# A graph attention and expert kernel: edge lists per pair of nodes instead of per node, with a buffer for every row tile

## The chip, the cores and the metric

The kernel runs on one core of a Trainium2 chip. The metric is the device time in microseconds (us) of one execution; lower is better. The engines named below are TensorE (PE; its weight loads are shown as PEld), VectorE (DVE), ScalarE (ACT), GpSimd (POOL) and SyncE (SP). Each takes its own instructions in order. DMA transfers are issued from SP, ACT and POOL, and those that gather rows by an index held in memory come from POOL.

## The reference, cut to what matters

1250 nodes with 768 features pass through two graph attention layers over 41250 edges (20000 drawn ones in both directions and one loop per node; the edges come sorted by destination), each layer adding a further loop per node, and then through a transformer block with attention and a routed mixture of experts.

```python
def _gat_layer(x, W, a_src, a_dst, b, src, dst, n_nodes):
    h = x @ W
    e_src = h @ a_src
    e_dst = h @ a_dst
    e = leaky_relu(e_src[src] + e_dst[dst], 0.2)
    m = segment_max(e, dst, num_segments=n_nodes)
    w = exp(e - m[dst])
    z = segment_sum(w, dst, num_segments=n_nodes)
    alpha = w / z[dst]
    return segment_sum(h[src] * alpha[:, None], dst, num_segments=n_nodes) + b

gnn = gat(relu(gat(layernorm(x), ...)), ...)      # two layers
x = x + gnn
x = x + ffn(layernorm(x))                         # attention, then 8 experts, 2 per row
```

The change lies wholly in the part ahead of the first layer's weighted sum.

## The kernel before, in words

**Counts instead of edges.** The kernel never sums over edges. It makes a dense table `cnt[source, destination]` of how often each edge occurs (125 x 10 x 1250, 16-bit) and uses it as a factor of a dense weight matrix. Nodes are cut into ten tiles of T = 125. The features of the nodes, layer-normalised, are held transposed in `xT`.

**How the lists are found.** Every edge gets a key, destination x 1250 + source (`key`, 125 rows of 330). The keys are stored to a DRAM array `keys`, with a tail of large values behind them. For a node, `find_rows` counts with a comparison (`begun`) and a one-column product (`pk`) in which row of 330 keys its edges start; `gather_row` fetches that row of keys for each of 125 nodes by an indirect DMA of POOL (`kr`); `first_edges` counts on DVE how many keys of the row lie before the node, and gathers the next SL = 64 keys from there (`win`). So there is one list of 64 per node, and each tile of 125 nodes costs two indirect DMAs. `gather_row` runs LEAD = 3 tiles ahead.

**How the lists become counts.** Two tiles at a time are transposed (`pl`), which gives 128 partitions (two lists of 64) by 625 columns (`lt`). A source node is split into tile number (`jb`) and place in the tile (`pb`); for the second list of a column the tile number is shifted by 10 (`shift`). For groups of PG = 25 columns DVE compares `pb` with 0 to 127 (`ohp`, 128x3200) and, every fifth group, `jb` with 1 to 20 (`ohj`, 128x2500); PE then makes, for every column, one product of the two (`pc`, 128x20), 25 to a group, 25 groups. ACT copies each group into `cnt`, one copy for each of the two lists (L423). `ohp` and the product's PSUM tile have two buffers each. If a list doesn't hold all the edges, a loop (L434) counts them in another way instead; with the drawn edges it makes no turn.

**What else goes on there.** A row tile of x is loaded (`xn`, four buffers; in a 112-row and a 13-row piece), its mean and spread are taken (`spread`), it is normalised (`normal`, on ACT), transposed on PE (`ptr`, six products of 128x125) and copied into `xT` (`columns`). The weight W1 (`gw`) is loaded in one DMA of 2304 KB. Three of the ten tiles of h = xW (`ph`, `project`, EARLY = 3) are computed between the row tiles, and seven after the counts. Of the scores e_src and e_dst only the vectors W a are formed: `attention_vectors` multiplies the six chunks of W with the vector spread over all partitions (`rep`) on DVE and sums (`scr`, twelve instructions, result `wa1`), one or two after each tile's list. `attention_terms` multiplies `wa1` with `xT` on PE (`pe`, three column chunks of six products), twelve before the counts and the rest one after every fourth group of counts; `pec` brings the result to rows (`es`).

**After the counts** the ones of the loops are added (L454), a mask `am` and the row maximum `most` are formed on DVE, transposed (`pmx`), turned into factors (`pes`, `rows`), and ten weight tiles `wt` are made on ACT and DVE; with them and h the weighted sum `pagg` starts.

**The order** on PE, DVE and POOL is written out by hand up to the end of the row tiles, and on PE and DVE in the counts (`manual_schedule`); elsewhere a scheduler orders them. Operations marked `keep_in_program_order`, some DMAs here, are not moved.

```python
for t in range(NT):
    if 2 <= t <= 7:
        spread(t + 2)
    first_edges(t)
    if t + LEAD < NT:
        gather_row(t + LEAD)
    if t % 3 == 0 and t // 3 < EARLY:
        project(xT, gw, h, gpo, [t // 3])
    vector(0 if t < 3 else 1 if t < 5 else 2)
    if 2 <= t <= 7:
        normal(t + 2)
        columns(t + 2)
```

Of the kernel before, what the change touches and what calls it, by code (L numbers as in the profile page):

```python
# [27 lines left out]
def gnn_ffn_kernel(  # L28
# [39 lines left out]
    SL = 64  # L68
    NP = N // 2
    PG = 25  # L70
# [9 lines left out]
    assert EC * T == E and EC % EB == 0 and 2 * SL == P and T % PG == 0 and NT % 2 == 0  # L80
# [79 lines left out]
    with tc.tile_pool(name="cnt", bufs=1) as cpool:  # L160
# [11 lines left out]
        def attention_vectors(layer, w, a_src, a_dst, pool, bufs, tags=("rep", "scr")):  # L172

            def load(a):
                rep = pool.tile([P, D], F32, tag=tags[0], name="rep", bufs=bufs if layer == 0 else None)
                tc.keep_in_program_order((nc.sync if bufs > 1 else nc.scalar).dma_start(
                    rep, bass.AP(tensor=a.tensor, offset=a.offset, ap=[[0, P], [1, D]])))
                return rep

            reps = [load(a) for a in (a_src, a_dst)[:bufs]]  # L180
            if bufs > 1:
                yield None
            for i in range(2):
                if i == bufs:
                    reps.append(load(a_dst))
                for c in range(DC):
                    scr = pool.tile([P, D], F32, tag=tags[1], name="scr", bufs=1 if layer == 0 else None)
                    nc.vector.scalar_tensor_tensor(scr, w[:, c, :], 1.0, reps[i], op0=ALU.mult, op1=ALU.mult,
                                                   accum_out=wa1[:, c, i:i + 1] if layer == 0 else wa2[:, i, c:c + 1])
                    yield None  # L190

        def attention_terms(xT, psum):

            for c0, w in CHUNKS:
                pe = psum.tile([P, 4, P], F32, tag="tr", name="pe").rearrange("p a b -> p (a b)")
                for c in range(DC):
                    g = c % 4
                    nc.tensor.matmul(pe[32 * g:32 * g + 32, :w], wa1[:, c, :], xT[:, c, c0:c0 + w],
                                     start=(c < 4), stop=(c + 4 >= DC))
                    if c == DC - 1:  # L200
                        nc.scalar.copy(er[:, c0:c0 + w], pe[:, :w])
                    yield None
# [17 lines left out]
        LEAD = 3  # L220
        with tc.tile_pool(name="edge", bufs=1) as ep, \
                tc.tile_pool(name="onehot", bufs=2) as op, \
                tc.tile_pool(name="epc", bufs=2, space=PSUM) as epc, \
                tc.tile_pool(name="gpt0", bufs=2, space=PSUM) as gpt, \
                tc.tile_pool(name="gpo0", bufs=2, space=PSUM) as gpo:

            ri = ep.tile([T, 2, EC], I32, name="ri")
            for i, (eng, a) in enumerate(((nc.sync, dst), (nc.scalar, src))):
                eng.dma_start(ri[:, i, :], a.rearrange("(p e) -> p e", p=T))
            xrows = []  # L230
            for t in range(4):
                xn = op.tile([T, D], F32, tag="xn", name="xn", bufs=4)
                split_rows(nc.sync if t % 2 == 0 else nc.scalar, xn, x[t * T:(t + 1) * T, :])
                xrows.append(xn)
            key = ep.tile([T, EC], F32, name="key")
            nc.vector.scalar_tensor_tensor(key, ri[:, 0, :], float(N), ri[:, 1, :], op0=ALU.mult, op1=ALU.add)
            tail = ep.tile([1, SL], F32, name="tail")
            nc.vector.memset(tail, 2.0 * N * N)
            nc.scalar.dma_start(keys[E:E + SL].rearrange("(o e) -> o e", o=1), tail)
            tc.keep_in_program_order(nc.sync.dma_start(keys[0:E].rearrange("(p e) -> p e", p=T), key))  # L240
            gw = wpool.tile([P, DC, D], F32, tag="w", name="gw1")
            tc.keep_in_program_order(nc.sync.dma_start(gw, gW1.rearrange("(c p) f -> p c f", p=P)))
# [6 lines left out]
            node = ep.tile([T, NT], F32, name="node")  # L249
            nc.gpsimd.iota(node, pattern=[[T, NT]], base=0, channel_multiplier=1,  # L250
                           allow_small_or_imprecise_dtypes=True)
            nc.vector.tensor_scalar(node, node, float(N), None, ALU.mult)
# [8 lines left out]
            shift = ep.tile([P, 1], F32, name="shift")  # L261
            nc.gpsimd.memset(shift, 1.0)
            nc.gpsimd.memset(shift[SL:P], 1.0 + NT)


            begun = ep.tile([T, N], BF16, name="begun")
            oneb = ep.tile([T, 1], BF16, name="oneb")
            nc.vector.memset(oneb, 1.0)
            row = ep.tile([T, NT], I32, name="row")
            edges = ep.tile([T, NT], F32, name="edges")  # L270
            at = ep.tile([T, NT], I32, name="at0")
            win = ep.tile([T, NT, SL], F32, name="win")
            krows = {}

            def find_rows():
                nc.vector.tensor_scalar(begun, nodes, head, None, ALU.is_gt)
                pk = epc.tile([P, 512], F32, tag="pc", name="pk")
                for t in range(NT):
                    nc.tensor.matmul(pk[:T, t:t + 1], begun[:, t * T:(t + 1) * T], oneb,
                                     start=True, stop=True)  # L280
                return pk

            def gather_row(t):
                krows[t] = op.tile([T, EC], F32, tag="kr", name="kr", bufs=LEAD)
                nc.gpsimd.indirect_dma_start(
                    out=krows[t], out_offset=None, in_=keys[0:E].rearrange("(p e) -> p e", p=T),
                    in_offset=bass.IndirectOffsetOnAxis(ap=row[:, t:t + 1], axis=0))

            def first_edges(t):

                count = small.tile([T, 1], F32, tag="count", name="count")
                nc.vector.scalar_tensor_tensor(key, krows[t], node[:, t:t + 1], ones[:T, :],
                                               op0=ALU.is_lt, op1=ALU.mult, accum_out=count)
                nc.vector.tensor_tensor(at[:, t:t + 1], count, edges[:, t:t + 1], ALU.add)
                nc.gpsimd.indirect_dma_start(
                    out=win[:, t, :], out_offset=None, in_=keys.rearrange("(e o) -> e o", o=1),
                    in_offset=bass.IndirectOffsetOnAxis(ap=at[:, t:t + 1], axis=0))
# [10 lines left out]
            xT = big.tile([P, DC, N], F32, tag="A", name="xnT")  # L308
            h = node_rows("h1")

            stats = {}

            def spread(t):
                if t == len(xrows):
                    xn = op.tile([T, D], F32, tag="xn", name="xn", bufs=4)
                    split_rows(nc.sync if t % 2 == 0 else nc.scalar, xn, x[t * T:(t + 1) * T, :])
                    xrows.append(xn)
                stats[t] = ln_root(xrows[t])

            def normal(t):  # L320
                mean, sd = stats.pop(t)
                rstd = small.tile([T, 1], F32, tag="rstd", name="rstd")
# [15 lines left out]
            with tc.manual_schedule(engines=fixed):  # L338
# [14 lines left out]
                for t in range(4):  # L353
                    columns(t)
# [755 lines left out]
```

## Time and profile before

| what | value |
|---|---|
| median of three runs (lowest, highest) | 1528.72 us (1525.68, 1529.65) |
| the profiled execution's own time, its span | 1527.86 us, 1526.1 us |
| PE, DVE, ACT, POOL busy of the span | 94%, 53%, 39%, 28% |
| first `ohj`, end of the last count copy | 70.29 us, 131.22 us |
| first `ph` after the counts, first `pagg` | 132.68 us, 195.61 us |
| `ph` products: 240 tile products' records, before and after the counts | 72 and 168 |

The span is the time from the first to the last instruction of one profiled execution, so it is a little shorter than that execution's own time. Busy shares are averages over stages with different limits. A group in the page is one source line on one engine: with its count, its busy time, the mean of one in ns, the idle time just before it and what ended that. The two records of one 32-bit product are counted singly, so that a `ph` tile of twelve products has 24 records.

### The profile page before, as it was taken

How to read it: one execution, taken by the hardware profiler on the slowest of the kernel's cores; microseconds unless marked ns; L12 is line 12 of the kernel's file. 1: busy time of each engine (PE TensorE's matmuls, PEld its weight loads, DVE VectorE, ACT ScalarE, POOL GpSimd, SP SyncE). 2: the span in 40 equal slices, each digit the busy share in tenths (PEclk: the TensorE clock that was granted, in tenths of full speed). 3: DMA queues.
4: the chain of work that ended last, by engine and by line, in shares of the span. 5: the costliest groups of instructions: out<-in, count | busy, mean ns of one | idle time of the engine just before them, and what ended most of it. 6: DMA issues, size and time to landing. Idle time of an engine off the chain costs nothing.

```text
span 1526.1 us, 15935 instructions
## 1 busy us (share of the span) xinstructions
PE 1442.0 (94%) x5957; PEld 781.8 (51%) x5957; DVE 813.5 (53%) x1326; ACT 598.0 (39%) x949; POOL 433.7 (28%) x288
## 2 busy tenths in 40 slices
PE   5699999999999999999999999999989996899998
PEld 3476655556555555553343343344333664566665
DVE  4797655435036650128778778778787764111111
ACT  3321613205116521236646646646656344221211
POOL 6300000000000010006646656655657222122222
PEclk9856999999999999999999999999999997899999
DMA  7100010000031129920000000000120433855644
GB/s 216 33 2 12 11 73 0 1 19 14 0 103 41 61 82 395 407 100 1 21 0 1 21 1 21 1 21 1 29 73 1 143 112 113 299 169 174 223 152 143
DMA packets 48848, 125.50 MB, mean 82 GB/s; under 512 B 6103, under 2 KB 22680, under 8 KB 48768
## 3 DMA queue, kind: packets, MB, share of 16 engines
q1 hardware_dynamic: 30958, 55.99, 11.0%
q0 software_dynamic: 12688, 57.10, 10.0%
q10 hardware_dynamic: 5122, 11.36, 2.6%
q8 instruction: 48, 0.79, 0.2%
q14 instruction: 32, 0.26, 0.1%
HBM read 71.30 MB, written 57.60 MB: 84 GB/s over the span
## 4 chain that ended last, share of the span: by engine, by line
PE 71%; DVE 9%; issue 8%; DMA 6%; ACT 4%; POOL 1%; POOLq 0%; SPq 0%; ACTq 0%; DVEq 0%
PE pagg L542 12%; PE ph L209 9%; PE st L694 8%; PE pav L738 7%; PE pk L657 5%; PE pv L673 5%; PE phe L1024 5%; PE poe L1033 5%; PE pq L657 4%; PE pc L419 2%; DMA xd<-yn,slot 2%; DVE sT L724 2%; PE po L882 2%; ACT sT L697 1%; DVE most L703 1%
## 5 line engine op out<-in xcount | busy, mean ns | idle before, releaser
L730 POOL TENSOR_TENSOR acc<-acc,sT 125x834 f32<-125x834 f32 (+1 forms) x139 | 273.0, 1964 | 10.9
L542 PE MATMUL pagg<-h,wt 125*125 125x385 f32 (+1 forms) x800 | 263.5, 486 | 0.4 <-DVE wt L535 0.4
L703 DVE TENSOR_TENSOR most<-most,st 125x834 f32<-125x834 f32 (+1 forms) x144 | 147.0, 1021 | 107.2 <-ACT sT L697 103.4
L542 PEld LDWEIGHTS pagg<-h,wt 125*125 125x125 f32 x800 | 147.1, 187 | 104.6 <-DVE wt L535 3.5
L724 DVE TENSOR_TENSOR sT<-sT,mb 125x834 f32<-125x834 f32 (+1 forms) x180 | 174.2, 1016 | 22.6 <-PE mb L719 22.6
L725 ACT ACTIVATE sT<-sT 125x834 f32<-125x834 f32 (+1 forms) x180 | 158.4, 900 | 49.3 <-DVE sT L724 49.0
L697 ACT COPY sT<-st 125x834 f32<-125x834 f32 (+1 forms) x180 | 151.5, 848 | 53.2 <-PE st L694 51.2
L694 PE MATMUL st<-qk 64*125 64x417 f32 (+1 forms) x720 | 164.9, 558 | 4.3 <-DVE most L703 4.2
L738 PE MATMUL pav<-sT,v 125*64 125x417 f32 (+1 forms) x720 | 151.8, 534 | 9.5 <-ACT sT L725 9.5
L635 POOL MEMSET zero<- 128x772 f32 x1 | 0.7, 741 | 505.9 <-PE ptr L140 505.9
L730 POOL TENSOR_TENSOR acc<-sT 125x834 f32<-125x834 f32 (+1 forms) x18 | 35.3, 1962 | 277.0 <-ACT sT L725 277.0
L694 PEld LDWEIGHTS st<-qk 64*125 64x125 f32 x720 | 56.9, 185 | 99.7 <-issue 43.2
L738 PEld LDWEIGHTS pav<-sT,v 125*64 125x64 f32 x720 | 42.8, 137 | 106.3 <-issue 43.8
L1033 PE MATMUL poe<-we,hT 128*128 128x384 f32 x264 | 88.8, 486 | 0.0
L657 PE MATMUL pq<-yT,wqk 128*128 128x417 f32 (+1 forms) x216 | 88.1, 534 | 0.0
L1037 DVE SCALAR_TENSOR_TENSOR sofar<-poe,weight,sofar 128x768 f32<-128x768 f32 x25 | 25.4, 1017 | 117.0 <-PE poe L1033 109.4
L882 PE MATMUL po<-wp,aT 128*125 128x384 f32 x240 | 87.5, 498 | 0.0
L209 PE MATMUL ph<-gw,xnT 128*125 128x384 f32 x240 | 85.5, 517 | 2.1 <-DVE cnt L454 2.1
L1024 PE MATMUL phe<-xT,we 128*128 128x384 f32 (+1 forms) x288 | 86.6, 460 | 0.0
L657 PE MATMUL pk<-yT,wqk 128*128 128x417 f32 (+1 forms) x216 | 84.0, 526 | 0.0
L673 PE MATMUL pv<-wv,yT 128*125 128x384 f32 x240 | 79.9, 490 | 1.4 <-issue 1.4
L546 DVE RECIPROCAL rz<-pagg 125x1 f32<-125x1 f32 x20 | 3.3, 166 | 141.5 <-PE pagg L542 141.5
(224 smaller groups left out, 1813.4 us busy)
## 6 DMA issues: line engine op xcount, KB each, us to landing
xd<-zero POOLq DMA_DIRECT2D x8, 3860.0 KB, 47.1
we<-in_L_ffn_W_dram SPq DMA_DIRECT2D x16, 1152.0 KB
xr<-xd SPq DMA_DIRECT2D x25, 386.0 KB
gw<-in_L_gnn_W_dram SPq DMA_DIRECT2D x2, 2304.0 KB
wqk<-in_L_ffn_Wqkv_dram SPq DMA_DIRECT2D x12, 384.0 KB
xres<-in_x_dram SPq DMA_DIRECT2D x10, 375.0 KB
xsd<-xres ACTq DMA_DIRECT2D x10, 375.0 KB
wv<-in_L_ffn_Wqkv_dram SPq DMA_DIRECT2D x1, 2304.0 KB
```

The lines of the kernel that those rows point to most:

```text
L209: nc.tensor.matmul(po[:, s, :DH], xT[:, c, t * T:(t + 1) * T], w[:, c, s * DH:(s + 1) * DH], start=(c == 0), stop=(c == DC - 1))
L542: nc.tensor.matmul(po[:, s, :DH + s], ws[j][:, (d - d0) * T:(d - d0 + 1) * T], h[:, j, s * DH:(s + 1) * DH + s], start=(j == 0), stop=(j = ...
L657: nc.tensor.matmul(pq[:, :w], wqk[:, c, i, :], yT[:, c, c0:c0 + w], start=(c == 0), stop=(c == DC - 1))
L694: nc.tensor.matmul(st[:T, i, :w], self.qk[r, 1, j * T:(j + 1) * T], self.qk[r, 0, self.c0:self.c0 + w], start=True, stop=True)
L697: nc.scalar.copy(s[:, :, :w], st[:T, :, :w])
L703: nc.vector.tensor_tensor(self.most[:, :, :w], prev[:, :, :w], st[:T, :, :w], ALU.max)
L724: nc.vector.tensor_tensor(s[:, :, :w], s[:, :, :w], self.mb[:T, :, :w], ALU.subtract)
L725: nc.scalar.activation(s[:, :, :w], s[:, :, :w], AF.Exp)
L730: nc.gpsimd.tensor_tensor(self.acc[:, :, :w], prev[:, :, :w], s[:, :, :w], ALU.add)
L738: nc.tensor.matmul(self.pav[r, :w], v[:, j, hd0:hd0 + HD], s[:, i, :w], start=(j == 0), stop=(j == NT - 1))
L1024: nc.tensor.matmul(ph[:, :n * P], w1[:, c, f * P:(f + 1) * P], xT[:, c, :n * P], start=(c == 0), stop=(c == DC - 1))
L1033: nc.tensor.matmul(po[:, d, :DH], hT[:, f, s * P:(s + 1) * P], w2[:, f, d * DH:(d + 1) * DH], start=(f == 0), stop=(f == FC - 1))
```

## The change

Every list now belongs to a pair of neighbouring nodes and has SL = 128 places. There are NU = 5 sets of 125 pairs instead of ten of 125 nodes. A source in a pair's list already carries the second node's offset of ten tiles, so `shift` is dropped, and a group's counts are copied to `cnt` in one copy of 50 columns instead of two of 25. All five `kr` gathers are issued at once.

Row tiles of x and gathered key rows have a buffer each, in a pool that closes before the counts. Edge lists and the key store are each sent in a 112-row and a 13-row piece (`queue`); the key store moves from SP's queue to ACT's, behind row tile 1; W1 stands on SP's queue behind row tiles 0, 2 and 3; row tiles 4 to 9 follow it there. `op`, the pool of the comparisons, opens after the row tiles, and `rep` is loaded then. The row tiles, lists and `ph` products are written in another order. `attention_vector` and `attention_terms` for layer 1 stand behind the counts and the loops' ones.

```diff
-    SL = 64
+    SL = 128
+    NU = NT // 2
...
+        def attention_vector(layer, i, w, rep, pool, tag):
+            for c in range(DC):
+                scr = pool.tile([P, D], F32, tag=tag, name="scr")
+                ins = nc.vector.scalar_tensor_tensor(
+                    scr, w[:, c, :], 1.0, rep, op0=ALU.mult, op1=ALU.mult,
+                    accum_out=wa1[:, c, i:i + 1] if layer == 0 else wa2[:, i, c:c + 1])
+                if layer == 0:
+                    tc.keep_in_program_order(ins)
...
+            def queue(eng, o, i):
+                for rs in (slice(0, 112), slice(112, T)):
+                    tc.keep_in_program_order(eng.dma_start(o[rs], i[rs]))
...
             for i, (eng, a) in enumerate(((nc.sync, dst), (nc.scalar, src))):
-                eng.dma_start(ri[:, i, :], a.rearrange("(p e) -> p e", p=T))
...
-            tc.keep_in_program_order(nc.sync.dma_start(keys[0:E].rearrange("(p e) -> p e", p=T), key))
-            gw = wpool.tile([P, DC, D], F32, tag="w", name="gw1")
-            tc.keep_in_program_order(nc.sync.dma_start(gw, gW1.rearrange("(c p) f -> p c f", p=P)))
+                queue(eng, ri[:, i, :], a.rearrange("(p e) -> p e", p=T))
...
+            with tc.tile_pool(name="early", bufs=1) as xp:
+                xrows = [xp.tile([T, D], F32, name=f"xn{t}") for t in range(NT)]
+                krows = [xp.tile([T, EC], F32, name=f"kr{u}") for u in range(NU)]
+                queue(nc.scalar, xrows[1], x[T:2 * T, :])
+                queue(nc.scalar, rows, key)
+                for t in (0, 2, 3):
+                    queue(nc.sync, xrows[t], x[t * T:(t + 1) * T, :])
+                tc.keep_in_program_order(nc.sync.dma_start(gw, gW1.rearrange("(c p) f -> p c f", p=P)))
+                for t in range(4, NT):
+                    queue(nc.sync, xrows[t], x[t * T:(t + 1) * T, :])
...
+                    for u in range(NU):
+                        nc.gpsimd.indirect_dma_start(
+                            out=krows[u], out_offset=None, in_=rows,
+                            in_offset=bass.IndirectOffsetOnAxis(ap=row[:, u:u + 1], axis=0))
...
+                    for t in range(4, NT):
+                        if t < 4 + NU:
+                            first_edges(t - 4)
+                        spread(t)
+                        if t > 4:
+                            normal(t - 1)
+                        if t % 2 == 0:
+                            project(xT, gw, h, gpo, [t // 2 - 2])
+                        if t > 4:
+                            columns(t - 1)
+                    normal(NT - 1)
+                    columns(NT - 1)
...
+            op = edge.enter_context(tc.tile_pool(name="onehot", bufs=2))
+            reps = [every_partition(a, op, "rep", nc.sync) for a in (ga_src1, ga_dst1)]
...
-            nc.vector.tensor_scalar(jb, jf, shift, good, ALU.add, ALU.mult)
+            nc.vector.tensor_scalar(jb, jf, 1.0, good, ALU.add, ALU.mult)
...
-                    u, q0 = divmod(g * PG, T)
-                    for i in range(2):
-                        c0 = (2 * u + i) * T + q0
-                        nc.scalar.copy(cnt[:, :, c0:c0 + PG],
-                                       pc[:T, :, i * NT:(i + 1) * NT].rearrange("p q j -> p j q"))
-                    if g % 4 == 3:
-                        next(terms, None)
-            for _ in terms:
-                pass
+                    c0 = 2 * g * PG
+                    nc.scalar.copy(cnt[:, :, c0:c0 + 2 * PG],
+                                   pc[:T].rearrange("p q (i j) -> p j (q i)", i=2))
...
             for t in range(NT):
                 d = cnt[:, t, t * T:(t + 1) * T]
                 nc.vector.tensor_tensor(d, d, ident[:T, :T], ALU.add)
+            for i, a in enumerate(reps):
+                attention_vector(0, i, gw, a, op, "scr")
+            attention_terms(xT, gpt)
```

## The prediction

> **What bounds the kernel now.** I read the chain of waits first, cut to the first 200 us (start, length, who holds the chain): everything the change touches lies ahead of the first `pagg` at 195.61 us, and behind it both programs issue the same work.
>
> ```profile
> 28.58 1.20 POOL win L295
> 29.78 0.30 issue
> 30.08 1.49 POOL kr L285
> ...
> 33.38 5.51 DMA kr<-keys,row
> ...
> 48.77 9.85 PE ph L209 x24
> ...
> 62.32 3.01 PE pe L198 x24
> ...
> 81.09 1.52 PE pe L198 x2
> ...
> 165.29 30.32 PE ph L209 x94
> 195.61 16.14 PE pagg L542 x50
> ```
>
> Three stretches. Up to 70.29 us (first `ohj`) the chain goes round between POOL, DMA and DVE, and PE is fed late. From there to 131.22 us it alternates between `ohp` (DVE) and `pc` (PE), with `pe` thrown in. From 132.68 to 195.61 us it is PE alone. The windows (busy us of each engine, granted clock, DMA share, GB/s) show their limits:
>
> ```profile
> 21.00:28.00 7.00, 7.00 (x23) 4.29 (x24) 1.21 (x4) 0.93 (x2) 3.11 (x3) 1.00 0.91 201
> 70.00:131.00 61.00, 53.93 (x637) 44.47 (x637) 53.71 (x32) 16.45 (x51) 0.00 (x0) 0.50 0.01 1
> ...
> 139.00:196.00 57.00, 56.99 (x205) 34.94 (x205) 36.62 (x53) 25.05 (x41) 0.00 (x0) 1.00 0.03 8
> ```
>
> In the second row PE and DVE are each busy 54 of 61 us, so neither hides the other; PE has half the clock. In the third PE is full while DVE has 20 us free. The timeline gives the hand-over between them:
>
> ```profile
> 131.64 2.08 DVE L454 TENSOR_TENSOR cnt<-cnt,ident 125x125 uint16<-125x125 uint16 x10 [3.85 <-ACT cnt L423]
> 132.51 0.50 ACTq L484 DMA_DIRECT2D bias<-in_L_gnn_b_dram  x1
> 132.68 0.49 PEld L209 LDWEIGHTS ph<-gw,xnT 128*125 128x125 f32 x2 [2.24 <-issue]
> ```
>
> PE takes up `ph` 1.46 us after the last count is copied out. That start is what the change moves.
>
> **What the Trainium skill says.** "TensorE: Matmul & The Clock Gate", section on the HAM clock gate: the array falls to half clock after an idle window of about 3.4 us and needs a busy one to come back. The trace agrees: 0.50 in 46 to 52 us after PE's pauses, 0.50 through the counts, back at 138.1 us, 5.4 us after `ph` starts. Same page, architectural detail: DVE and ACT are strictly first in, first out; so an operation queued ahead of what PE needs holds it. "DMA: Bandwidth & Descriptors", "Why a DMA increments its semaphore by 16": a copy takes the largest k up to 16 that divides its outer dimension, so 125 rows use 5 engines and 112 use 16. No row splits a transfer by engine, but one-piece `ri` lands only at 7.5 us. Same page, "Issuing engines are not separate DMA queues": all share the 16 engines; the trace agrees, the gathers land after 4.2 us at best and 10.8 at worst, when they run against `gw`.
>
> **The change, part by part.** Durations are of the profiled execution, span 1526.10 us, own time 1527.86, 0.86 below the median of the three runs, 1528.72; I add the difference to the median.
>
> 1. Start. `ri` (2 x 161 KB) and the key store go out in 112 and 13 rows. `key` starts at 7.54 now; estimate 5.0 (bounds 5.0 to 7.5). The key store leaves SP (issued at 9.58, 1.5 after `key` is done) for ACT's queue behind x row 1: about 6; ACT issues seven loads and stores ahead of its first activation instead of six, 0.3 to 0.4 more, while it waits for DVE's first `mv` anyway. First gather at 14.96 now, estimate 10 to 11.4. On SP `gw` now stands behind six pieces of x rows 0, 2, 3 (0.3 to 0.4 each, and the waits for earlier loads): issue at about 8 against 9.89. Rows 4 to 9 follow it on SP without waiting for buffers (now issued at 15.4 to 45.8).
>
> 2. Lists. Five `kr` (1.28) and five `win` (1.21) gathers fewer: POOL 12.5 us less; DVE 5 x (0.56 + 0.08 + 0.16) = 4.0 less. Half the bytes of `kr` (825 KB), the same bytes of `win`. `begun` halves (0.87 to about 0.5 to 0.9, strided), five `pk` fewer (0.12 each). This frees the chain of 28 to 47 us: DVE then needs neither 12 `scr` (12.0) nor ten lists before the last row.
>
> 3. The front on PE, by its own order: four tiles of transposes, `ph` 0, row 4, `ph` 1, rows 5 and 6, `ph` 2, rows 7 to 9, `psum`, `pl`. `gw` is 2304 KB; at 400 GB/s it lands near 17 to 18, at the 201 GB/s of the window in which gathers run, nearer 22. I take `ph` 0 at 20 (21.56 now). One `ph` tile is 24 records of 30.32 / 94 = 0.323 = 7.75 us warm (now 8.2, 9.2 and 10.0, two of them after a pause and partly at half clock). 20.0 + 7.75 + 0.6 cold = 28.3; row 4, 1.2; `ph` 1 to 37.3; rows 5 and 6 with their evictions, 2.1; `ph` 2 to 47.2; rows 7 to 9, 3.7: 50.9. From `pl` to `ohj` stays 66.33 to 70.29 = 3.96. `ohj` starts at **54.9 instead of 70.29: 15.4 less** (11 to 18).
>
> 4. Counts. Twelve `pe` products (3.01) leave the front, six of 1.52 leave the counts, 9.1 us of PE. What remains on PE, 25 x 1.85 = 46, is below DVE's 25 x 1.89 + 5 x 1.46 = 54.5; so DVE bounds: 54.5 + last `pc` 1.86 + copy 0.6 + hand-overs 0.5 = 57.4 against 60.93: **3.5 less** (1.5 to 4). Fifty count copies of 0.32 become 25 of about 0.57 (an ACT copy of 125x500, `rows`, takes 0.57); ACT is at 16 of 61 us, so only the last one shows. `rf` (0.49) moves to a DVE that waits for PE anyway.
>
> 5. Behind the counts. Let T be the end of the last copy, 131.22 now. DVE: diagonal until T+2.5, then the twelve `scr`, which DVE issues ahead of all else, at 1.00 each (204.84, 205.84 in layer 2): T+14.5. PE issues all 18 `pe` ahead of the remaining `ph`; the first needs the seventh `scr`, the sixth the twelfth. So 168 `ph` records stand behind DVE. Then 12 `pe`, 3.0 warm to 6 at half clock; `er` copy and the last `pec`, 1.5. `ph` starts at about T+20.5 (19.3 to 22.3), not T+1.46. What follows: 168 x 0.323 = 54.2, and `pmx` and `pes` as now, 139.00 to 195.61 less 160 records and `pec`, 3.6: `pagg` at T+78.3 against T+64.4: **13.9 more** (12.7 to 16). DVE's own chain, ten `am` ahead of `es`, `most`, then the first `wt` row, ends near T+57, inside that. `rep` now loads after the x rows have left their buffers, near 50 us, and is wanted at about 115: the counts, with DMA at 1 GB/s, hide it; without them it would cost 3 to 5 us.
>
> Sum: -15.4 - 3.5 + 13.9 = -5.0; 1526.1 becomes 1521.1, the execution 1522.9, the median 1523.7.
>
> **The rivals.** *A draw.* With both gathers and loads at 200 to 220 GB/s the front gains only 11, the counts 2.5, and PE's stall costs 15: +1.5; or kinder, 12.5, 3 and 14: -1.5. For it: 201 GB/s at a DMA share of 0.91 above. Against it: half the gather bytes. It gives 1526 to 1530.
>
> *Slower: the gathers starve.* DVE's order puts the first list's count, which waits for `krows[0]`, ahead of row 4's statistics. Rows 0 to 9, `gw` and five gathers now compete from 8 us on. If `kr` lands at L, row 4 is ready for PE at L + 0.8 + 1.25 + 0.8 + 1.25 + 0.6 + 1.0 = L + 5.7; PE wants it at 28.3, so each us of L beyond 22.6 is lost. At 27.6 the gain is gone, from 32.2 the kernel is slower by over 0.3%. For it: 10.8 us to landing in the trace, and 8.4 us of DVE waiting for the first `kr`. Against it: issue is 4 us earlier, and 4.5 MB at 300 GB/s are through by about 26. With L at 34: 1535.
>
> *More gain.* `gw` lands at 17.5 and PE is warm: front -18, counts -4, stall +13: -9, 1520.
>
> *It doesn't do what it says:* a pair with more than 128 edges would send all counting through the loop of L434. The drawn destinations give 66 edges a pair on average and 96 at most: excluded.
>
> **How the numbers follow.** About 0.3%, 4.6 us, is what a measurement of this kernel can tell from no change. The forecast, 0.45, runs over 1519 to 1527 and lies on that bound; the draw has 0.25, more gain 0.18, starving 0.12. Faster by over 0.3% (under 1524.1): more gain and somewhat over two thirds of the forecast, 0.5. Within 0.3%: the rest of it, the draw, and a mild starving, 0.37. Slower: 0.13. The range 1516 to 1531 leaves out the far ends of more gain and of starving.
>
> **What would show it.** Right: `ohj` at 52 to 58 us; no `pe` between two `pc` and 57 us from `ohj` to the last count copy; PE idle for some 8 us after the counts, then waiting on `scr`, `ph` 19 to 22 us after the last copy; `pagg` at 188 to 193. Wrong: a long DVE wait for the first `kr`, or PE taking `ph` before `pe`; the forecast falls if `ohj` comes after 60 us or if the stages behind 200 us last other than now by over 2 us.

## The result, and the profile after

The changed kernel takes **1522.79 us** (median of eight runs, 1520.32 to 1528.96), the kernel before 1529.38 (eight runs): ratio 0.9964, 95% interval 0.9952 to 0.9977. Measured a second time (e5 below, 21 runs beside 32 of the kernel before) it is 1526.07 against 1528.69, ratio 0.9982 [0.9973, 0.9991]. So the gain is real, between 0.1 and 0.5%, and lies on the bound of what one measurement tells apart, as forecast. The profiled execution has a span of 1520.5 us (before: 1526.1) and an own time of 1522.34.

First the chain of waits of the changed kernel up to 200 us (start, length, who holds it):

```profile
112.13 0.48 ACT cnt L406
...
113.20 2.08 DVE cnt L433 x10
115.28 6.17 DVE scr L182 x14
121.45 0.04 issue
121.49 8.24 PE pe L194 x36
129.73 2.29 PE pec L473 x20
...
154.89 35.48 PE ph L204 x110
190.37 9.69 PE pagg L524 x30
```

The last count copy ends at 112.71 (T; 131.22 before). Then DVE, not PE, holds the chain until 121.49 (the diagonal and the first seven `scr`), and `pagg` starts at 190.37 against 195.61. The windows (busy us of PE, PEld, DVE, ACT and POOL with instructions in brackets, granted clock, DMA share, GB/s) show the same three stretches as before, and a new one between the second and the third:

```profile
20.00:30.00 10.00, 10.00 (x27) 5.57 (x26) 6.90 (x25) 2.82 (x6) 4.79 (x5) 1.00 0.99 227
60.00:110.00 50.00, 43.00 (x592) 41.22 (x590) 48.55 (x28) 13.29 (x23) 0.00 (x0) 0.50 0.01 2
114.00:125.00 11.00, 3.51 (x10) 0.73 (x10) 11.00 (x30) 0.00 (x0) 0.00 (x0) 0.50 0.01 1
135.00:190.00 55.00, 54.75 (x190) 32.79 (x189) 31.58 (x43) 24.45 (x39) 0.00 (x0) 1.00 0.03 8
```

In the front PE is now full while the DMA engines are full too. In the counts DVE is busy 48.6 of 50 us, so it alone is the bound; before, PE and DVE had 54 of 61 each. From 114 to 125 DVE is full while PE works for 3.5 of 11 us, all of it on `pe` after 121.49: that is the stall that the change brings in. The timeline has the steps:

```profile
3.10 4.81 POOL L250 IOTA lane<- 128x3200 bf16 x1
...
5.65 2.62 DVE L288 TENSOR_SCALAR begun<-nodes,head 125x625 bf16<-125x625 f32 x1
...
19.32 10.54 PE L204 MATMUL ph<-gw,xnT 128*125 128x384 f32 x24 [0.51 <-DMA gw<-in_L_gnn_W_dram]
...
30.34 7.91 PE L204 MATMUL ph<-gw,xnT 128*125 128x384 f32 x24
...
55.93 1.47 DVE L397 TENSOR_TENSOR ohj<-jb,upto 128x2500 bf16<-128x2500 bf16 x1
...
112.13 0.58 ACT L406 CAST cnt<-pc 125x500 uint16<-125x500 f32 x1 [1.45 <-PE pc L404]
...
121.49 8.24 PE L194 MATMUL pe<-xnT,wa 128*32 128x417 f32 x36 [9.39 <-DVE scr L182]
131.86 15.08 PE L204 MATMUL ph<-gw,xnT 128*125 128x384 f32 x46
```

The bracket at the end of a line is the idle time before it and what ended it: `pe` waited 9.39 us for `scr`.

### The profile page after: what moved, and what is told of

Same layout as the page of the kernel before. It is cut to its first block, busy times and chain, and to the rows that moved or that the text cites. A ratio compares the mean times of both kernels' runs of the same rounds, so it can differ in the third digit from the quotient of the medians.

```text
span 1520.5 us, 15858 instructions
## 1 busy us (share of the span) xinstructions
PE 1433.7 (94%) x5952; PEld 779.0 (51%) x5952; DVE 811.9 (53%) x1311; ACT 595.6 (39%) x924; POOL 418.6 (28%) x276
## 4 chain that ended last, share of the span: by engine, by line
PE 67%; DVE 9%; issue 7%; ACT 4%; DMA 4%; POOL 1%; POOLq 0%; SPq 0%; ACTq 0%; DVEq 0%
PE pagg L524 13%; PE st L676 8%; PE ph L204 7%; PE pav L720 7%; PE pk L639 5%; PE pv L655 5%; PE phe L1006 5%; PE poe L1015 5%; PE pq L639 4%; DMA xd<-yn,slot 2%; DVE sT L706 2%; PE po L864 2%; ACT sT L679 1%; DVE most L685 1%; PE mb L701 1%
## 5 line engine op out<-in xcount | busy, mean ns | idle before, releaser
L204 PE MATMUL ph<-gw,xnT 128*125 128x384 f32 x240 | 81.4, 498 | 0.5 <-DMA gw<-in_L_gnn_W_dram 0.5
```

Of the source, the lines that this page charges most:

```text
L204: nc.tensor.matmul(po[:, s, :DH], xT[:, c, t * T:(t + 1) * T], w[:, c, s * DH:(s + 1) * DH], start=(c == 0), stop=(c == DC - 1))
```

## The experiments

Each was timed beside the kernel before on its own chip (e1 to e4 on one, e5 to e8 on a second, e9 to e11 on a third, e12 on a fourth), so across chips the ratios are compared and not the times. The other columns, in us, are of one profiled execution each. T is the end of the last count copy; `pagg` is its start in the chain.

| kernel | ratio to before, interval | first `ph` | `ohj` | T - `ohj` | `pagg` - T | `pagg` |
|---|---|---|---|---|---|---|
| before | 1 | 21.56 | 70.29 | 60.93 | 64.39 | 195.61 |
| changed | 0.9964 [0.9952, 0.9977] | 19.32 | 55.93 | 56.78 | 77.66 | 190.37 |
| e5, changed again | 0.9982 [0.9973, 0.9991] | 20.15 | 55.65 | 56.79 | 78.29 | 190.73 |
| e2, late vectors alone | 1.0023 [1.0015, 1.0031] | 21.72 | 65.11 | 56.86 | 78.62 | 200.59 |
| e1, vectors early | 0.9964 [0.9955, 0.9974] | 19.62 | 64.18 | 56.78 | 64.72 | 185.68 |
| e6, the same with a buffer | 0.9905 [0.9888, 0.9922] | 24.73 | 60.67 | 56.81 | 65.93 | 183.41 |
| e7, six terms in the counts | 0.9939 [0.9925, 0.9953] | 23.82 | 60.12 | 60.86 | 65.80 | 186.78 |
| e10, e6 with five row buffers | 0.9973 [0.9959, 0.9988] | 19.15 | 56.51 | 67.25 | 64.98 | 188.74 |

### The stall behind the counts: e2, e1, e6

**e2_late_vectors_alone** puts only this part of the change into the kernel before (`lt`, not shown, gets another buffer).

```diff
-                    vector(0 if t < 3 else 1 if t < 5 else 2)
...
-                terms = attention_terms(xT, gpt)
-                for _ in range(2 * DC):
-                    next(terms)
...
-                    if g % 4 == 3:
-                        next(terms, None)
...
+            for _ in vectors:
+                pass
+            for _ in attention_terms(xT, gpt):
+                pass
```

> The kernel before with one part of the change alone: the twelve scr and 18 pe behind the counts; lists per node, loads and order of the rest as before. Theory: behind the counts the same 13 us are lost as in the changed kernel (first pagg 77 to 78 us after the last count copy instead of 64.4); the counts shorten by 3.5 to 4 and the front by the 3.0 us of pe and perhaps 1 to 3 of DVE, so the kernel is 4 to 6 us slower than before, 1533 to 1535. Rival (the late vectors are what pays, since they free DVE and PE at the front): faster than before.

Measured: 1533.34 us, 0.23% slower; that is 3.8 us, just under the 4 to 6 that were expected. The timeline of e2 after the counts:

```profile
131.41 8.53 PE L200 MATMUL pe<-xnT,wa 128*32 128x417 f32 x36 [10.12 <-DVE scr L188]
```

The same 10 us of PE waiting for `scr` stand behind the counts. The table splits the move: the front gives 70.29 - 65.11 = 5.2 us, the counts 4.1, and the stretch from T to `pagg` takes 14.2. The net, +5.0 at `pagg`, is 4 in the medians. So this part alone is a loss; the rest of the change has to carry it.

**e1_vectors_in_gap** takes it out of the changed kernel: the twelve `scr` stand behind the last operation on `win`, where DVE has nothing to do from 38.4 to 51.6 us, and the 18 `pe` behind `pl`.

```diff
                     queue(nc.sync, xrows[t], x[t * T:(t + 1) * T, :])
+                reps = [every_partition(a, ep, f"rep{i}", nc.sync) for i, a in enumerate((ga_src1, ga_dst1))]
...
             nc.vector.tensor_scalar(wf, wf, -FAR, None, ALU.add)
+            for i, a in enumerate(reps):
+                attention_vector(0, i, gw, a, op, "scr")
...
+            attention_terms(xT, gpt)
             jf = op.tile([P, NP], F32, name="jf", bufs=1)
```

> The changed kernel with the twelve scr placed on DVE right after the list work (DVE idles there from 38.4 to 51.6 us) and all 18 pe placed on PE behind pl (PE idles there from 52.8 to 59.3 us); rep is loaded behind the x rows with buffers of its own. Theory (PE stands behind DVE's vectors after the counts): ph starts 1.5 us after the last count copy instead of 19.1, the pe cost nothing in their new place (18 x 0.25 = 4.5 us warm in a gap of 6.4), the first pagg comes 13 us earlier, near 177, and the kernel is 13 us faster than the changed one, about 1510. Rival 1 (the time behind the counts is the pe and pec products' own, cold array included, and not the wait): they cost as much in the new place, gain under 5 us. Rival 2 (the array goes cold in the wait and would otherwise be warm): ph shows the half clock for 5 us as in the kernel before, gain 10.5 instead of 13.

Measured: 1524.18 us, the ratio of the changed kernel, where 13 us less were expected. The stall is gone (`ph` 1.5 us behind T, `pagg` at T+64.7), but `ohj` comes 8.25 us later. DVE's timeline tells why:

```profile
50.81 0.96 DVE L182 SCALAR_TENSOR_TENSOR scr<-gw,rep 128x768 f32<-128x768 f32 x1 [10.59 <-PE ptr L141]
```

`scr` needs nothing from a row's transposes (`ptr`); its buffer does. Pool `op` takes over the memory of the closed pool `early`, so the first write into it waits for the last row tile to be read. Most of the gain was turned into a wait for a buffer. (`pagg` still starts 4.7 us earlier, in a profile of the fastest of e1's runs. There the chain then hangs on the load of the second layer's weights, 8.46 us from 185.68, so part of this is lost again.)

**e6_vectors_own_buffer** changes that one thing (the new place has one buffer for `scr` instead of two):

```diff
-                attention_vector(0, i, gw, a, op, "scr")
+                attention_vector(0, i, gw, a, ep, "scr")
```

> The vectors and terms again ahead of the counts, as in e1, but `scr` has a buffer of its own, so that it no longer waits for the x rows' memory. Theory (the stall behind the counts and the buffer wait of e1 are the whole story, and DVE's idle stretch of 38.4 to 51.6 us is free): twelve `scr` of 0.88 run from 38.5 to 49; 36 `pe` records run behind `pl` in PE's idle stretch of 53 to 59 in 4.2 to 5; `ohj` stays at 56 to 57; last count copy at 112.5 to 114; `ph` 1.5 us behind it, `pagg` at T+64.7, so at 177 to 179, 11 to 13 less than in the changed kernel; of that 2 go again to the load of the second layer's weights as in e1: span near 1510, ratio near 0.989. Rival (PE has no room there: the terms delay the count's first products, or the copies of `er` stand ahead of `lt` on ScalarE): `ohj` or the first `pc` 4 us or more later, ratio 0.992 to 0.995. Second rival (DVE reads `gw` in PE's busy stretch and is slowed, or the loads of `rep` come late): `scr` ends past 53, `ohj` later than 59.

Measured: **1513.71 us**, 12.4 less than e5 on the same chip, ratio 0.9905 where about 0.989 was expected; it is the fastest of all. DVE's and PE's timelines of e6:

```profile
43.81 0.95 DVE L182 SCALAR_TENSOR_TENSOR scr<-gw,rep 128x768 f32<-128x768 f32 x1
...
58.10 4.39 PE L194 MATMUL pe<-xnT,wa 128*32 128x417 f32 x36 [0.60 <-ACT lt L383]
...
119.00 5.35 PE L204 MATMUL ph<-gw,xnT 128*125 128x384 f32 x8 [2.14 <-DVE cnt L437]
```

`scr` starts as soon as the last operation on `win` has ended, with no wait. `pe` takes 4.39 us instead of 8.24, in a pause of PE, and `ph` follows T by 1.5 us. The numbers of this profile are 5 us later than expected from `ohj` on, since its `gw` landed late (24.7, more on that below); it was the slowest of the five runs of e6. So `pagg` is only 7.3 us earlier than in e5's profile, where 11 to 13 were expected.

### What the counts cost: e7, and by accident e10

**e7_six_terms_in_counts** is e6 with the last chunk of `pe` back where the kernel before has it.

```diff
-            attention_terms(xT, gpt)
+            terms = attention_terms(xT, gpt)
+            for _ in range(2 * DC):
+                next(terms)
...
+                    if g % 4 == 3:
+                        next(terms, None)
```

> e6_vectors_own_buffer, with the last of the three chunks of `pe` (6 products, 12 records) put back among the counts, one product behind every fourth group of five, as the kernel before had it. Theory (they hold the counts up: the counts took 60.9 us before and 56.8 after): from `ohj` to the last copy 60 to 61 us instead of 56.8, `pagg` and the kernel 3 to 4 us later than e6. Rival (DVE's 48.6 busy of 50 us sets the counts alone, and the 4 us went with the copies, of which there were 50 and are 25): under 57.5 us, the kernel within 1 us of e6.

Measured: 1520.36 us; the counts take 60.86 us, against 56.81 in e6 and 60.93 before. (The medians of e7 and e6, of five runs each, lie 6.65 us apart and the spans of their profiles 3.1; the counts explain 4.) Its chain shows how six products of 1.5 us cost 4 us although DVE is the busier engine:

```profile
111.48 1.90 DVE ohp L407
113.38 0.05 issue
113.43 3.64 PE pc L411 x50
117.07 1.53 PE pe L194 x2
118.59 1.79 PE pc L411 x25
```

A likely reason, argued and not tried, is that with two `ohp` buffers DVE can't run far ahead of a PE that is held up, so part of each `pe` reaches the chain. The other candidate, 50 count copies against 25, is excluded: e2 has all 50 and takes 56.86.

**e10_own_buffer_five_rows** was meant for the next question.

> e6_vectors_own_buffer and e9_five_row_buffers together, with the two loads of `rep` behind row 9's. Theory: the gains add: `gw` at 17.5 to 20, `scr` from 39 to 50, `ohj` at 55 to 57, T at 112 to 114, `ph` 1.5 us behind, `pagg` at 177 to 179, ratio 0.987 to 0.9895, and the runs closer together than those of e6 (1511 to 1519). Rival (row 9 and `rep` come too late for DVE, which runs `scr` into the time of `good` and `jf`): `scr` ends past 54, `ohj` at 58 or later, ratio 0.990 to 0.993.

Measured: 1524.23 us. It missed both: `ohj` is at 56.51 but T at 123.76. The place of `scr` on DVE is the scheduler's here. With the loads of `rep` later (probably for that reason) it put two `scr` between `pb` and `ohj` and the other ten among the `ohp`, instead of all ahead of them, as DVE's timeline shows:

```profile
58.77 1.89 DVE L416 TENSOR_TENSOR ohp<-pb,lane 128x3200 bf16<-128x3200 bf16 x1
60.57 0.95 DVE L182 SCALAR_TENSOR_TENSOR scr<-gw,rep 128x768 f32<-128x768 f32 x1
61.44 0.08 DVE L182 DVE_READ_ACCUMULATOR scr<-gw,rep 128x1 f32 x1
61.44 1.89 DVE L416 TENSOR_TENSOR ohp<-pb,lane 128x3200 bf16<-128x3200 bf16 x1
```

The counts grew by 10.4 us. The ten `scr` in them are 10 x 0.88 = 8.8 of that; the rest goes with the `pe`, which came to stand in the counts too, and for which DVE waits twice, 0.93 and 1.52 us. The total says nothing on row buffers, but what is put on DVE in the counts shows in full.

### The front: e8, e3, e4, e9, e11, e12

**e5_changed_again** is the changed kernel itself beside e6, e7 and e8.

> The changed kernel as it is, on the chip of the next three, so that they can be compared with it. Both theories expect a ratio of about 0.9965 to the kernel before, `ohj` near 56, the last count copied out near 112.7, `ph` 19 us behind that, `pagg` near 190.4.

Measured: `ohj`, T, `ph` at T+18.6 and `pagg` as expected, but a ratio of 0.9982 instead of 0.9965. The difference lies behind `pagg` (see what stays open).

**e8_loads_in_one_piece** undoes the 112/13 pieces of `ri` and of the key store.

```diff
-                queue(eng, ri[:, i, :], a.rearrange("(p e) -> p e", p=T))
+                tc.keep_in_program_order(eng.dma_start(ri[:, i, :], a.rearrange("(p e) -> p e", p=T)))
...
-                queue(nc.scalar, rows, key)
+                tc.keep_in_program_order(nc.scalar.dma_start(rows, key))
```

> The changed kernel with the two edge lists and the key store each moved by one copy of 125 rows instead of copies of 112 and 13. Theory (the pieces make `key` and its store early, and the first list's gather waits for that store): `key` at 7.0 to 7.6 instead of 4.74, `begun` ending at most 1 us later since it ends at 8.3 anyway, the first `kr` gather 2.5 to 5 us later than 10.5, landing at 21 to 24 instead of 18.6; row 4 has 2.5 us to spare at PE, so `ohj` comes 0 to 3 us later, ratio 0.9965 to 0.9985. Rival (nothing waits for the store; the gather follows `row`): the first gather under 1 us later, `ohj` as before within 0.5.

```profile
7.74 0.50 DVE L234 SCALAR_TENSOR_TENSOR key<-ri 125x330 f32<-125x330 int32 x1 [6.66 <-DMA ri<-in_dst_dram]
...
8.65 0.55 DVE L288 TENSOR_SCALAR begun<-nodes,head 125x625 bf16<-125x625 f32 x1
...
10.84 0.11 DVE L326 TENSOR_SCALAR row<-pk 125x5 int32<-125x5 f32 x1
...
14.66 1.38 POOL L329 DMA_INDIRECT kr<-keys,row  x1 [6.75 <-DMA xn<-in_x_dram]
```

`key` is 3.0 us later than in the changed kernel, `row` 1.5, and the first gather 4.1: it goes out 3.8 us after `row`, so it waits for something later. The key store is what the gather reads, and the gather follows its issue by 5.0 to 6.4 us in the kernel before, the changed one, e3 and e8, while its distance to `row` runs from 1.2 to 3.8. In e3 `row` comes at 9.00 and the gather still at 10.50. That part of the theory holds, though no view shows the landing of the store itself. The time, 1526.73 us, ratio 0.9988 [0.9979, 0.9997], is 0.7 us above e5 and the intervals overlap: no difference is measured, so the earlier gather brings 0.7 of its 4.1 us at best guess. (In the profile `ohj` is at 61.07, but that profile again has a late `gw`, 24.6. From the first `ph` to `ohj` it takes 36.5 us, as in the changed kernel.)

**e3_lane_late** issues POOL's fill of `lane` (4.8 us) behind the `kr` gathers instead of ahead.

```diff
-            nc.gpsimd.iota(lane, pattern=[[1, P], [0, PG]], base=0, channel_multiplier=0,
-                           allow_small_or_imprecise_dtypes=True)
...
+                    nc.gpsimd.iota(lane, pattern=[[1, P], [0, PG]], base=0, channel_multiplier=0,
+                                   allow_small_or_imprecise_dtypes=True)
                     nc.gpsimd.iota(upto, pattern=[[1, 2 * NT], [0, 5 * PG]], base=1, channel_multiplier=0,
```

> The changed kernel with POOL's iota of lane (4.81 us, 3.1 to 7.9) moved behind the five key row gathers. In the changed kernel begun takes 2.62 us and the tiny pair 2.47, both ending as that iota ends. Theory (DVE's two instructions are held while POOL works, so the earlier key bought nothing there): begun falls to 0.4 to 0.9 us and row is ready by 7.5 to 8.5 instead of 9.4; the first gather still waits for the stored keys and starts at 9.5 to 10.5, and rows 0 to 3 wait for their loads, so the whole moves by 0 to -1 us. Rival (begun is slow by its stride of two): begun stays at 2.6 us. Rival for the total: the front hangs on row, 1.5 us or more faster.

```profile
5.66 0.17 DVE L244 TENSOR_SCALAR pair<-pair 125x5 f32<-125x5 f32 x1
5.84 0.55 DVE L286 TENSOR_SCALAR begun<-nodes,head 125x625 bf16<-125x625 f32 x1
```

`pair` falls from 2.47 us to 0.17 and `begun` from 2.62 to 0.55, so it was `lane` that held them. `row` gains only 0.35 us, since the spread of row tile 0 stands ahead of it on DVE. Nothing comes of it, 0.9976 [0.9969, 0.9983]: the gather doesn't follow `row`, and on POOL `lane` and `upto` now stand ahead of the first `win` gather, at 25.39 instead of 20.67.

**e4_warm_array** adds 15 products of 125x330, whose result nothing reads, to PE between 4 and 18 us.

```diff
+                    warm(8)
                     pk = find_rows()
+                    warm(4)
                     spread(0)
...
                         columns(t - 1)
+                        warm(1)
```

> The changed kernel with 15 products on PE whose results are not used (125x330 of ones), 8 from 2 us on, 4 behind pk, one after each of the first three row tiles. In the changed kernel the first ph takes 10.5 us, its records 0.64 us apart until 24.5 us and 0.32 after that, against 7.75 warm. Theory (the array is cold when the first ph starts, so the forecast's 0.6 us for that was 2 us too small): the first ph takes 7.8 to 8.2 us, ohj comes 2 to 2.8 us earlier unless row 4 (normalised at 26.9) then holds PE, and the kernel gains 1.5 to 2.5 us. Rival (the first ph is slow because gw and x still stream in, DMA at 1.0 of its share): it stays at 10.5.

Measured: 1527.1 us, 0.9987 [0.9979, 0.9995], no gain. The transposes ran in 0.9 us instead of 1.5, but the first `ph` tile still took 9.70 us (10.54 in the changed kernel's profile, 9.43 in e5). Windows of e4 and then of the changed kernel:

```profile
21.50:24.50 3.00, 3.00 (x6) 1.48 (x5) 1.82 (x6) 0.59 (x3) 0.62 (x1) 0.50 1.03 228
24.50:30.00 5.50, 5.50 (x18) 3.16 (x17) 3.18 (x12) 1.65 (x4) 2.04 (x2) 1.00 1.04 210
```

```profile
20.50:23.50 3.00, 3.00 (x6) 1.50 (x5) 1.82 (x6) 0.29 (x1) 1.21 (x1) 1.00 1.02 238
25.00:28.00 3.00, 3.00 (x11) 1.74 (x10) 2.54 (x10) 1.21 (x2) 1.19 (x1) 1.00 1.04 234
```

Both run six `ph` records in the first 3 us shown, and the pace rises by 1.6 to 1.8 times after that (18 in 5.5, 11 in 3). The DMA engines are full in all four windows, so the loads that still stream in, the rival, are not what makes the first ones slow. Thin work did not keep the array warm: e4's clock falls to 0.50 within the first microsecond of `ph`. The Trainium skill ("TensorE: Matmul & The Clock Gate", section "What's actually happening", on the clock gate) lets it fall after an idle window of about 3.4 us. Here PE was never idle that long: its longest pause, the wait for `gw`, was 1.73 us. In the 2.4 us up to `ph` it was busy for 0.74. So a thinly filled stretch was enough; where the bound lies, and which products count, these runs don't show.

**e9_five_row_buffers** undoes "a buffer for every row tile" by half.

```diff
-                xrows = [xp.tile([T, D], F32, name=f"xn{t}") for t in range(NT)]
+                    xrows[t] = xp.tile([T, D], F32, tag="xn", name="xn", bufs=5)
...
                     transpose_rows(gpt, xrows[t], evict_to(xT, t))
+                    load(t + 5)
```

> The changed kernel with five buffers for the x rows instead of ten, so that row 5 is loaded when row 0 is transposed (near 14), row 6 near 15.5, row 7 near 17, row 8 near 19 and row 9 after row 4's transposes (near 30). In the profiles so far of kernels with the changed kernel's front the first `ph` waited for `gw` until 19.3, 19.6, 20.2, 23.8 and 24.7, and `ohj` came at 55.7 to 55.9 with the early and at 60.1 to 60.7 with the late ones. Theory (rows 4 to 9, 2.25 MB queued right behind `gw`, share the DMA engines with it, and whether `gw` or they come first differs from run to run): `gw` lands at 17.5 to 20 in the profile, `ohj` at 54 to 56, the runs lie closer together, ratio 0.994 to 0.9965. Rival (it is the gathers that `gw` shares with, or the late rows then hold DVE's order up): `gw` at 19 to 25 as before, or `ohj` later than 57; ratio 0.998 to 1.000.

Measured: 1527.04 us (1522.66 to 1530.38), 0.9987 [0.9979, 0.9995]; first `ph` at 20.76, `ohj` at 56.86. The theory falls: the runs spread as far as those of e5 (1522.6 to 1530.24) and the time is no better, nor is it worse, so half of the row buffers bring nothing that was measured. Rows 5, 6 and most of 7 still came onto the queue ahead of the landing of `gw` (SP issues them from 14.1 to 18.0 us), so it is not excluded that they compete; five buffers don't prevent it.

**e11_own_buffer_gw_ahead** is e6 with the load of `gw` ahead of row tiles 2 and 3 on SP.

```diff
-                for t in (0, 2, 3):
+                queue(nc.sync, xrows[0], x[0:T, :])
+                tc.keep_in_program_order(nc.sync.dma_start(gw, gW1.rearrange("(c p) f -> p c f", p=P)))
+                for t in (2, 3):
                     queue(nc.sync, xrows[t], x[t * T:(t + 1) * T, :])
-                tc.keep_in_program_order(nc.sync.dma_start(gw, gW1.rearrange("(c p) f -> p c f", p=P)))
```

> e6_vectors_own_buffer with the load of `gw` queued on SP ahead of x rows 2 and 3 instead of behind them, 1.6 us earlier; all ten row buffers stay. Theory (what counts is what shares the DMA engines with `gw`, not when it is issued): `gw` issued near 6.8 and landing at 18 to 23, row 2 or 3 up to 3 us later on PE, ratio within 0.002 of e6. Rival (whoever is queued first lands first): `gw` at 16.5 to 18.5 always, `ph` at 18.5 to 19.5, `ohj` at 55 to 56, ratio 0.986 to 0.989.

Measured: 1517.5 us, 0.9924 [0.991, 0.9937], 0.0019 above e6, with intervals that overlap. PE's timeline:

```profile
19.66 1.51 PE L141 MATMUL ptr<-ident,xn 125*128 125x125 f32 x6 [5.06 <-ACT xn L319]
22.84 2.96 PE L141 MATMUL ptr<-ident,xn 125*128 125x125 f32 x12 [1.67 <-ACT xn L319]
25.60 8.41 PE L204 MATMUL ph<-gw,xnT 128*125 128x384 f32 x24
```

`ph` no longer waits for `gw`, but the rows behind it are late, and it starts at 25.6. With the DMA engines full, the order on the queue here only chose who is late.

**e12_gathers_twice** issues each `kr` gather twice, the second time into a buffer that nothing reads.

```diff
-                        nc.gpsimd.indirect_dma_start(
-                            out=krows[u], out_offset=None, in_=rows,
+                        for k in (krows, again):
+                            nc.gpsimd.indirect_dma_start(
+                                out=k[u], out_offset=None, in_=rows,
```

> The changed kernel with each of the five `kr` gathers issued twice, the second time into a buffer that nothing reads: 825 KB more between 10 and 27 us, and POOL busy with issuing until about 25 instead of 18. It prices the rival of the prediction in which the gathers starve. Theory (gathers, `gw` and x rows share one rate of about 230 GB/s while gathers run, and the front has 2 to 3 us to spare at row 4): 3.6 us more to move, `gw` lands at 22 to 28, `ohj` at 58 to 62, ratio 1.000 to 1.003. Rival (a gather costs what POOL takes to issue it, and its bytes move beside the rest): the first `ph` at 19 to 25 as in the other profiles, `ohj` at 56 to 60, ratio 0.997 to 0.9995.

Measured: 1527.35 us, 0.9994 [0.9986, 1.0003]; first `ph` 21.70, `ohj` 61.30. `ohj` is where the theory has it; the ratio and the first `ph` lie just outside its ranges and inside the rival's. DVE's waits up to 45 us (us in total, times, longest), first of e12, then of the changed kernel:

```profile
DVE key L300 <- DMA kr<-keys,row: 9.5, 4, 5.6
```

```profile
DVE key L299 <- DMA kr<-keys,row: 4.3, 1, 4.3
```

The counting of every list but one waits now, where only the first did. From the first `ph` to `ohj` it takes 39.6 us, against 35.5 to 36.6 in the changed kernel and in e3 to e9, so about 3 us are lost in the front. PE shows most of them as a wait of 2.34 us ahead of the transposes of row tile 6, at 43.29. The copies that it waits for stand on ACT behind the normalising of later rows, which DVE, held by the last lists, releases late. In time it is about 2 us beside e5, on another chip and with intervals that overlap. So the prediction's starving rival is real with twice the gathers. The run does not separate the bytes from the issuing: POOL takes 1.5 us for each gather, so that of the last list goes out at 22.83 instead of 16.74.

## Why the prediction was right, point by point

1. **Start.** `key` at 4.74 (forecast 5.0), first gather at 10.54 (10 to 11.4), `gw` issued at 8.47 (8). `begun` took 2.62 us, not 0.5 to 0.9; it cost nothing, since without that delay the first gather still goes out at 10.50 (e3).
2. **Lists.** As forecast, each stage once per pair. Taking e2's share out, as if the two simply add, the lists, loads and order of rows give 65.11 - 55.93 = 9.2 us of the front. No run splits this sum further. Undoing the pieces (e8) or half of the row buffers (e9) makes no measured difference, so that it is the fewer lists and the order is argued and not shown.
3. **Front.** `ohj` at 55.93 and, in e5, 55.65 (forecast 54.9). The term that was mis-sized is the cold start: 0.6 us were put down for it, but the first `ph` tile takes 10.54 us (9.43 in e5) against 7.91 for the two after it. `ph` 0 starting at 19.32 instead of 20 gave part of that back. Row 4 was ready at 26.93, 2.5 us before PE asked for it (29.4), so the gathers do not starve the front. But the rival's sum, L + 5.7, is too short: the first `kr` is there at L = 18.65, and row 4 comes at L + 8.3. What holds it are the loads of rows 4 and 5, which stand behind `gw` on SP's queue; DVE waits 2.00 us for the first and 1.06 for the second:

```profile
21.41 1.02 DVE L120 BATCH_NORM_STATS2 st<-xn 125x6 f32<-125x384 f32 x2 [2.00 <-DMA xn<-in_x_dram]
...
24.36 1.02 DVE L120 BATCH_NORM_STATS2 st<-xn 125x6 f32<-125x384 f32 x2 [1.06 <-DMA xn<-in_x_dram]
```

4. **Counts.** 56.78 us, 4.15 less than before; forecast 57.4 and 3.5 less. Mechanism right: e7 brings back 4.05 of it by six `pe`. The sum was 0.6 too high, mostly in the hand-overs: 0.5 us were put down for them, and 0.1 are there between the last `ohp`, `pc` and the copy.
5. **Behind the counts.** `ph` at T+19.15 (forecast 20.5), `pagg` at T+77.66 (78.3). `scr` takes 0.88 us here, not the 1.00 of layer 2: twelve of them are the 1.4 us. (In e6, with one buffer for `scr` instead of the two of e1, they start 1.00 us apart as well.) The order is as forecast, DVE ahead of PE, `pe` ahead of `ph`.

The sum was -5.0 at `pagg`; -5.24 is measured, and -4.88 in e5. The three terms are -14.4, -4.15 and +13.3 instead of -15.4, -3.5 and +13.9. Each is right to about 1 us, so it is no cancellation of large errors; but the errors (+1.0, -0.65 and -0.6) do cancel, and that the sum is right to 0.3 is partly luck. In time the medians moved by 6.6 us in the first measurement and by 2.6 in the second, around a forecast of 5.0. The two profiles differ behind `pagg`, a part that the forecast took as unchanged.

One reading of the prediction doesn't hold. It takes the half clock of the counts as agreeing with a fall after an idle window of about 3.4 us. But there PE is busy 43.0 of 50 us by its records and its longest pause is this one:

```profile
102.59 3.64 PE L404 MATMUL pc<-ohj,ohp 128*128 128x20 bf16 x50 [1.32 <-DVE ohp L400]
```

Still the clock stays at 0.50. The forecast doesn't rest on this, since it takes the durations in the counts from the trace.

**What stays open.** Behind `pagg`, where nothing was changed, the changed kernel's profile takes 1330.1 us to the end of the span (before: 1330.5), but e5's takes 1332.3 and e6's 1333.9. This accounts for most of the 2.5 us between the two spans of the same program. And the landing of `gw` lies anywhere from 19.3 to 24.7 us in kernels with the same front (changed, e1, e5, e6, e7), with `ohj` near 56 or near 60.5 when DVE's order is the same. What decides it, neither e9 nor e11 nor e12 could settle. Both profiles with five row buffers have it early (20.8 in e9, 19.2 in e10), but two profiles decide nothing.

## What to carry to other kernels

Split a change that moves work into what it frees and what it charges, and time the moved part by itself: here 13.3 of the 18.5 us won ahead of T went to a stall, for work that a free stretch of the same engine could have taken. Before filling a pause, look at what the operation's buffer waits for and at the order the scheduler gives it, not only at its data: e1 and e10 lost most of the same gain at a buffer and at a place in DVE's queue, and e6 kept it. Where the DMA engines were full, putting one load ahead of another (e11) or issuing a gather earlier (e8) only moved the wait.

## What the runs showed of the hardware that was not expected

- Some DVE operations that start while POOL fills a large tile end only after it. `pair` (125x5) and `begun` (125x625), both TENSOR_SCALAR, took 2.47 and 2.62 us while POOL's fill of `lane` ran from 3.10 to 7.91, and 0.17 and 0.55 us without it (e3); both took 0.17 and 0.55 in e8 as well, where they start after 7.91. `key`, a SCALAR_TENSOR_TENSOR, was not held: it took 0.50 us in the middle of the fill (from 4.74), and 0.50 in e3 without it. The Trainium skill has it: "SBUF — State Buffer", section on the two separate sides, calls the port pair that the two engines share an exclusive lock that the first one keeps for its whole instruction, and names only certain DVE operations as taking it.
- The clock column can be wrong at the start: it says 1.00 for 20.5 to 23.5 us of the changed kernel, where `ph` runs six records in 3 us, and 0.50 for a stretch of e4 with the same pace. The pace of the records is what to go by.
- The rate of full DMA engines differs by a factor of almost two. The DMA view of the changed kernel, up to 60 us (GB/s in 40 slices of 1.5 us):

```profile
GB/s 0 193 302 274 260 104 281 352 406 422 356 269 251 244 236 243 225 226 230 194 103 27 43 16 0 0 0 0 0 0 0 0 0 0 0 188 322 14 0 0
```

From 12 to 15 us they move 406 to 422 GB/s, from 18 to 28.5 only 225 to 251, with a share of 0.99 in 20 to 30 us. In the second stretch the gathered rows land, the first at 18.65 us. That they are the cause was not tried apart from e12, where the low rate (188 to 238) runs from 16.5 to 34.5 us.
